# Two of the four combined weight blocks summed on VectorE, one part at a time

## The chip, the cores and the metric

The kernel runs on one core of a Trainium2 chip. A core has a matrix engine (TensorE, PE in the profile), two elementwise engines (VectorE or DVE, ScalarE or ACT), GpSimd (POOL) and SyncE (SP). Here SP only issues DMAs, and POOL mostly issues those that add into their destination or gather rows. Each engine works through a queue of its own, in order; semaphores make one wait for another. The metric is the time of one execution in microseconds of device time. The kernel before took 430.67 us, the median of three runs (430.34 to 432.82).

## The reference

The input `x` is 64 samples of 64 rows and 1024 columns. Each sample picks one of 16 matrices by its condition, and its rows are mixed with it; the mixed rows then go through a dense layer with a mixture of four low-rank experts, and the result is added to `x`:

```python
u = einsum('bct,bcd->bdt', x, weights[condition])      # 64 x 64 per sample
logits = u @ gate_w.T + expert_bias                    # 4 experts
base = einsum('bth,oh->bto', u, W_up)                  # 1024 x 1024
z = einsum('nh,erh->ner', u, lora_A)                   # rank 8 per expert
d = einsum('ner,ehr->neh', z, lora_B)
out = x + base + (d of the expert with the largest logit)
```

All is float32.

## The kernel before

**Order of the algebra.** Mixing rows and multiplying columns commute. The kernel therefore multiplies `x` first with one wide weight matrix, `gate_w`, `lora_A` and `W_up` side by side (1024 x 1060), giving `u`, and mixes the rows of that afterwards, with the block-diagonal matrix `bd` of two samples. Two samples make a tile of 128 rows; there are 32 tiles, and two tiles make a group, so there are 16 groups.

**Precision.** Each operand is split in two parts, a rounded one (`h`, a cast on ACT) and the rest (`l`, a subtraction on DVE, which waits for that cast). A product of two operands is three matmuls: high by high, high by low, low by high. `split_a` (line 124) does this for blocks of `x`, `split_b` (line 141) for blocks of weights, `u_split` (line 186) for `u`.

**Blocks.** A group's 256 rows by 1024 columns of `x` are four blocks A11, A12, A21, A22 and the weights four blocks B11, B12, B21, B22 of 512 by 530. A block of weights is held and split in four parts `k` = 0 to 3, each 128 x 530, 265 KB. A product of two blocks (`product`, line 160) is four steps k of six matmuls, 24 in all. The first two groups need eight products each (`eight`, line 384). The other 14 groups need only seven (`seven`, line 498), by a scheme in the manner of Strassen and Winograd, which uses sums S1 to S4 of the x blocks, made on DVE for each group, and sums of the weight blocks, made once:

T1 = B12 - B11, T2 = B22 - T1, T3 = B22 - B12, T4 = B21 - T2.

These four are made while the first two groups run, since only the third group (`g == 2`) begins to use them: T2 in its second product, T1 in its third, T3 in its fifth, T4 in its seventh.

**How they are made.** `begin_b` (line 145) loads a part of a block into a temporary tile, on SP's queue. `next_b` (line 150) negates a tile in place on ACT and then has POOL issue a DMA that adds a part of another block to it, so every difference is a negation and an accumulating load. T1 starts from a load of B11, T3 from a second load of B12; T2 goes on in T1's tiles, and T4 in T2's. `split_b` then writes the two parts of the result, `hT` and `lT` in the profile. T4's split takes the place of B12's, which is no longer needed.

**Order of the work.** The order of PE, DVE, ACT and POOL is written out by hand: `InOrder` (line 33) keeps the program's order on each of them. In `eight` and `seven`, `at(s, k, fn, ...)` puts a piece of work behind step `k` of product `s` (k = -1: ahead of the product), and `each` does so for several parts. So a position such as (5, 2) says behind which matmuls on PE the work of PE is put, and in which order the other engines find theirs; ACT and DVE do not wait for PE there unless they read something of it. The order of SP's loads follows the program too, and a load waits until the tile that it overwrites is free.

**Around the products.** `u_of` (line 194) takes a finished product out of PSUM (ACT writes `uh`, DVE `ul`). `apply` (line 247) mixes rows: three small matmuls that read `uh` and `ul`. `gate` (line 257) finds the best expert on DVE in seven short instructions, from `lg` to `z`; `turn` (line 276) transposes its result on PE and splits it (`zt`, ACT and then DVE); `delta` (line 290) is one matmul of `zt` with the experts' matrix `b3`; `evict` (line 296) copies the output columns out of PSUM on ACT (`y`), and after a tile's third set of columns POOL adds `x` to it by an accumulating DMA and SP stores it. `finish` (line 311) is `apply`, `delta` and `evict` for one of three sets of columns. `split_b3` (line 366) splits `b3` after its load.

Every tile of weights, S or T is one of ten temporaries of one pool (`tp`, line 81), so a load can wait for an old tile to be read.

Of the kernel before, what the change touches and what calls it, by code (L numbers as in the profile page):

```python
# [17 lines left out]
KH = KC // 2  # L18
# [26 lines left out]
def kernel(  # L45
# [25 lines left out]
    nc = tc.nc  # L71
    NP = x.shape[0]
    NG = NP // 2
    tensor, vector, scalar, pool = (
        InOrder(tc, e) for e in (nc.tensor, nc.vector, nc.scalar, nc.gpsimd)
    )
# [17 lines left out]
    raw, As, us, ys, wsel, zs, os_, ts = ({} for _ in range(8))  # L94

    def temp(name):
        return tp.tile([P, NB], F32, name=name, tag="t")
# [35 lines left out]
    def part(q, k):  # L133
        i, j = int(q[1]) - 1, int(q[2]) - 1
        return w[j][:, KH * i + k]

    def load_b(q, k):
        t = raw[q, k] = temp("wraw")
        nc.sync.dma_start(t, part(q, k))  # L139

    def split_b(q, k):
        scalar.copy(wh[q][:, k], raw[q, k])
        vector.tensor_sub(wl[q][:, k], raw[q, k], wh[q][:, k].bitcast(F32))

    def begin_b(q, k, block):

        t = raw[q, k] = temp(q)
        nc.sync.dma_start(t, part(block, k))

    def next_b(q, k, block, of=None):  # L150

        t = raw[q, k] = raw[of or q, k]
        scalar.mul(t, t, -1.0)
        pool.dma_start(t, part(block, k), accum_op=ALU.add)


    def chain():
# [19 lines left out]
    def body(c):  # L177
        return c[:, LEFT : LEFT + NB]
# [7 lines left out]
    def u_split(i, n, src):  # L186
        h, lo = u_tiles(i)
        scalar.copy(h[:, n], src)
        vector.tensor_sub(lo[:, n], src, h[:, n].bitcast(F32))

    def half(hf):
        return slice(NB * hf, NB * hf + NB)

    def u_of(i, hf, c):
        u_split(i, half(hf), body(c))
# [5 lines left out]
    def u_sum(i, hf, c, t):  # L201
        u_add(i, c, t)
        u_split(i, half(hf), ts["u", i])
# [168 lines left out]
    def run(g, order, hooks, c):  # L372
        for s, (n, l, r, first) in enumerate(order):
            if first:
                c[n] = chain()
            for kk, fn, *args in hooks[s]:
                if kk < 0:
                    fn(*args)
            product(c[n], g, l, r, first, hooks[s])
# [4 lines left out]
    def eight(g):  # L384
        a, b = 2 * g, 2 * g + 1
        h = [[] for _ in range(8)]

        def at(s, k, fn, *args):
            h[s].append((k, fn, *args))

        def each(s, k, fn, q, ks, *args):
            for i in ks:
                at(s, k, fn, q, i, *args)

        one, two = (0, 1), (2, 3)
        if g == 0:
            at(0, 0, split_a, g, "A21")
            each(0, 1, split_b, "B21", one)
            at(0, 2, split_a, g, "A12")
            each(0, 3, split_b, "B21", two)  # L400
            each(1, -1, load_b, "B12", range(KH))
            at(1, 0, split_a, g, "A22")
            each(1, 1, split_b, "B12", one)
            each(1, 3, split_b, "B12", two)
            each(1, 3, load_b, "B22", range(KH))
            at(2, 1, split_cond, a)
            at(2, 2, load_b3)
            for i in (2, 3):
                at(2, 3, load_half, i, 0)
            at(3, -1, lambda: u_of(a, 0, c["1"]))  # L410
            at(3, 1, split_cond, b)
            each(3, 2, split_b, "B22", one)
            each(3, 2, begin_b, "T1", range(KH), "B11")
            at(3, 3, apply, a, 0)
            at(3, 3, gate, a)
            at(4, -1, lambda: u_of(b, 0, c["2"]))
            at(4, 1, split_b3)
            each(4, 2, split_b, "B22", two)
            at(5, 0, turn, a)
            each(5, 0, next_b, "T1", one, "B12")  # L420
            for i in (2, 3):
                at(5, 0, load_half, i, 1)
            at(5, 2, delta, a, 0)
            at(5, 2, evict, a, 0)
            at(6, 0, apply, b, 0)
            at(6, 0, gate, b)
            each(5, 3, next_b, "T1", two, "B12")
            at(5, 3, split_a, g + 1, "A11")
            each(5, 3, begin_b, "T3", range(KH), "B12")
            at(6, 2, split_a, g + 1, "A21")  # L430
            at(6, 3, turn, b)
            at(7, -1, lambda: u_of(a, 1, c["3"]))
            at(7, 1, delta, b, 0)
            at(7, 1, evict, b, 0)
            at(7, 1, split_a, g + 1, "A12")
            at(7, 2, finish, a, 1)
            each(7, 2, split_b, "T1", one)
            at(7, 3, finish, a, 2)
            order = (
                ("1", "A11", "B11", True),  # L440
                ("2", "A21", "B11", True),
                ("1", "A12", "B21", False),
                ("2", "A22", "B21", False),
                ("3", "A11", "B12", True),
                ("1", "A21", "B12", True),
                ("3", "A12", "B22", False),
                ("1", "A22", "B22", False),
            )
        else:
            p = a - 1  # L450
            at(0, -1, lambda: u_of(p, 1, cs[g - 1]["1"]))
            at(0, 0, split_a, g, "A22")
            at(0, 3, finish, p, 1)
            at(1, 0, finish, p, 2)
            each(0, 3, next_b, "T3", (0, 1, 2, 3), "B22")
            each(1, 1, split_b, "T1", two)
            at(1, 1, load_cond, a + 2)
            at(1, 1, load_cond, b + 2)
            for i in (b + 2, a + 2):
                at(1, 1, load_half, i, 0)  # L460
            each(1, 3, next_b, "T2", one, "B22", "T1")
            each(2, 1, next_b, "T2", two, "B22", "T1")
            for i in (b + 2, a + 2):
                at(2, 1, load_half, i, 1)
            at(3, -1, lambda: u_of(a, 1, c["1"]))
            each(3, 1, split_b, "T3", one)
            each(3, 3, split_b, "T3", two)
            at(4, -1, lambda: u_of(b, 1, c["2"]))
            at(4, 0, sums, g + 1, "S1")
            at(4, 1, split_cond, a)  # L470
            each(4, 1, split_b, "T2", one)
            each(4, 2, next_b, "T4", one, "B21", "T2")
            at(4, 3, split_cond, b)
            at(5, 0, sums, g + 1, "S2")
            each(5, 1, split_b, "T2", two)
            each(5, 2, next_b, "T4", two, "B21", "T2")
            at(5, 2, split_a, g + 1, "A11")
            at(5, 3, sums, g + 1, "S3")
            at(6, 1, split_a, g + 1, "S2")
            at(6, 2, sums, g + 1, "S4")  # L480
            at(7, -1, lambda: u_of(a, 0, c["3"]))
            at(7, 3, apply, a, 0)
            at(7, 3, gate, a)
            order = (
                ("1", "A11", "B12", True),
                ("2", "A21", "B12", True),
                ("1", "A12", "B22", False),
                ("2", "A22", "B22", False),
                ("3", "A11", "B11", True),
                ("1", "A21", "B11", True),  # L490
                ("3", "A12", "B21", False),
                ("1", "A22", "B21", False),
            )
        run(g, order, h, c)
        cs[g] = dict(c)


    def seven(g):
        a, b = 2 * g, 2 * g + 1
# [5 lines left out]
        def at(s, k, fn, *args):  # L505
            h[s].append((k, fn, *args))

        def each(s, k, fn, q, ks, *args):
            for i in ks:
                at(s, k, fn, q, i, *args)  # L510
# [15 lines left out]
        if g == 2:  # L526
            at(0, -1, lambda: u_of(pb, 0, cp["1"]))
            at(0, 2, turn, pa)
            at(1, 0, delta, pa, 0)
            at(1, 0, evict, pa, 0)  # L530
            at(1, 1, finish, pa, 1)
            at(1, 2, finish, pa, 2)
            each(1, 3, split_b, "T4", (0, 1))
            each(2, 3, split_b, "T4", (2, 3))
            at(1, 3, apply, pb, 0)
            at(1, 3, gate, pb)
            at(2, 3, turn, pb)
        else:
            at(0, -1, lambda: u_sum(pb, 0, cp["2"], ts["t1"]))
            at(0, 1, finish, pa, 1)  # L540
            at(0, 3, finish, pa, 2)
            at(1, 2, apply, pb, 0)
            at(1, 2, gate, pb)
            at(2, 2, turn, pb)
# [102 lines left out]
    for g in range(2):  # L647
        eight(g)
    for g in range(2, NG):
        seven(g)  # L650
# [44 lines left out]
```

## Time and profile before

| | us |
|---|---|
| median of three runs | 430.67 |
| the profiled execution | 433.13 |
| its span, first to last instruction | 431.1 |
| PE busy in it | 416.1 (97%) |
| DVE busy | 280.3 (65%) |
| ACT busy | 190.5 (44%) |
| POOL busy | 80.3 (19%) |
| DMA of POOL's queue | 21.13 MB, 29.0% of 16 engines' span |
| DMA of SP's queue | 41.53 MB, 27.1% of 16 engines' span |

The profile names instructions by what they write and read: `c<-hT,ah` is a product matmul into the accumulator `c`, `o<-uh,bd` a mixing matmul, `lT<-T,hT` the low part of a combined block. Nearly everything carries line 41, the helper that records it. The page divides the span into 40 slices and prints one digit for each, the busy share in tenths; for PEclk it is the clock that PE was granted. An answer on waits gives the waiting engine and its operation, who ended the wait, and the total, the number and the longest in us. An answer by stretches gives, for each stretch, its length, each engine's busy time with the number of instructions, the granted clock, the DMA share and GB/s. In the timeline a row is the start, the length, the engine, what it did, and in brackets how long the engine had been idle and who ended that.

### The profile page before, as it was taken

The numbers are of one execution on the slowest core, as the hardware profiler recorded it, in microseconds if no ns is written. First come the engines' busy times: TensorE is split into PE (matmuls) and PEld (weight loads), VectorE is DVE, ScalarE is ACT, GpSimd is POOL, SyncE is SP. The second block draws the span as 40 slices with busy tenths as digits, with TensorE's granted clock in tenths as the row PEclk, the third lists the DMA queues.
The fourth block names the chain that finished last, engine by engine and source line by source line (L and its number), as shares of the span: only waits on it lengthen the run. The fifth ranks groups of instructions, "written<-read, shape, count | busy, mean of one in ns | idle before, by whom it ended". The sixth has DMA issues, their size and how long they took to land.

```text
span 431.1 us, 8166 instructions
## 1 busy us (share of the span) xinstructions
PE 416.1 (97%) x3187; PEld 412.6 (96%) x3187; DVE 280.3 (65%) x631; ACT 190.5 (44%) x425; POOL 80.3 (19%) x97
## 2 busy tenths in 40 slices
PE   8979995999999999999999999999999999999996
PEld 6979995999999999999999999999999999999995
DVE  4855355677676766766676666667676666767656
ACT  5764753534353334435234444533444353433531
POOL 3330821302002020200202020110202011020000
PEclk9989997999999999999999999999999999999999
DMA  7999997445354654435465453546445344665343
GB/s 218 344 304 231 221 201 137 79 95 156 106 166 128 172 128 93 126 95 160 129 170 129 100 133 90 157 124 170 129 111 141 89 141 120 173 155 145 50 97 147
DMA packets 26598, 63.18 MB, mean 147 GB/s; under 512 B 3552, under 2 KB 4832, under 8 KB 26560
## 3 DMA queue, kind: packets, MB, share of 16 engines
q0 software_dynamic: 7680, 21.13, 29.0%
q1 hardware_dynamic: 18880, 41.53, 27.1%
q8 instruction: 25, 0.41, 0.4%
q14 instruction: 13, 0.11, 0.1%
HBM read 45.87 MB, written 16.78 MB: 145 GB/s over the span
## 4 chain that ended last, share of the span: by engine, by line
PE 80%; issue 8%; DMA 5%; POOL 3%; DVE 2%; SPq 1%; ACT 1%; POOLq 0%; DVEq 0%
PE c L41 67%; PE o L41 14%; DMA T<-in_w_dram 4%; POOL wsel L41 1%; POOL T L41 1%; DMA cond_sb<-in_cond_dram 1%; DVE lT L41 1%; SPq L327 0%; SPq L139 0%; DVE S L41 0%; ACT hT L41 0%; DVE y L41 0%; DVE al L41 0%; DVE usum L41 0%; DVE ul L41 0%
## 5 line engine op out<-in xcount | busy, mean ns | idle before, releaser
L41 PE MATMUL c<-hT,ah 128*128 128x264 f32 x480 | 140.3, 292 | 0.0
L41 PE MATMUL c<-lT,ah 128*128 128x264 f32 x480 | 137.8, 287 | 0.0
L41 PE MATMUL c<-hT,al 128*128 128x264 f32 x480 | 137.6, 287 | 0.0
L41 PE MATMUL c<-hB,ah 128*128 128x264 f32 (+1 forms) x432 | 125.9, 291 | 0.8 <-ACT ah L41 0.8
L41 PE MATMUL c<-hB,al 128*128 128x264 f32 (+1 forms) x432 | 125.3, 290 | 0.3 <-DVE al L41 0.3
L41 PE MATMUL c<-lB,ah 128*128 128x264 f32 (+1 forms) x432 | 125.0, 289 | 0.3 <-DVE lB L41 0.3
L41 PEld LDWEIGHTS c<-lT,ah 128*128 128x128 f32 x480 | 91.3, 190 | 0.0
L41 PEld LDWEIGHTS c<-hT,al 128*128 128x128 f32 x480 | 91.3, 190 | 0.0
L41 PEld LDWEIGHTS c<-hT,ah 128*128 128x128 f32 x480 | 91.3, 190 | 0.0
L41 PEld LDWEIGHTS c<-hB,ah 128*128 128x128 f32 x432 | 83.1, 192 | 1.5 <-ACT ah L41 1.2
L41 PEld LDWEIGHTS c<-lB,ah 128*128 128x128 f32 x432 | 83.3, 193 | 1.0 <-DVE lB L41 0.9
L41 POOL DMA_DIRECT2D y<-in_x_dram x30 | 28.9, 963 | 293.9 <-ACT y L41 293.9
L41 PEld LDWEIGHTS c<-hB,al 128*128 128x128 f32 x432 | 82.8, 192 | 0.6 <-DVE al L41 0.5
L41 ACT COPY y<-o 128x354 f32<-128x354 f32 (+2 forms) x90 | 39.9, 443 | 62.4 <-PE o L41 60.5
L41 DVE TENSOR_TENSOR al<-xh,ah 128x512 fp32r<-128x512 f32 (+1 forms) x53 | 34.9, 660 | 35.4 <-ACT ah L41 35.4
L41 ACT CAST uh<-usum 128x530 fp32r<-128x530 f32 (+4 forms) x44 | 27.1, 616 | 68.8 <-DVE usum L41 68.7
L41 DVE TENSOR_TENSOR al<-S,ah 128x512 fp32r<-128x512 f32 x56 | 38.5, 688 | 22.9 <-ACT ah L41 22.8
L41 PE MATMUL o<-uh,bd 128*128 128x354 f32 (+2 forms) x188 | 45.9, 325 | 4.0 <-ACT uh L41 3.9
L41 ACT CAST zt<-o 96x128 fp32r<-96x128 f32 x32 | 8.4, 262 | 83.2 <-PE o L41 83.2
L41 DVE TENSOR_TENSOR ul<-usum,uh 128x530 fp32r<-128x530 f32 (+4 forms) x44 | 30.0, 683 | 19.3 <-ACT uh L41 19.3
L41 POOL DMA_INDIRECT wsel<-in_cw_dram,idx x32 | 35.2, 1101 | 9.9 <-issue 4.9
L41 ACT CAST ah<-S 128x512 fp32r<-128x512 f32 x56 | 34.8, 623 | 0.3
(59 smaller groups left out, 461.6 us busy)
## 6 DMA issues: line engine op xcount, KB each, us to landing
xh<-in_xt_dram SPq DMA_DIRECT2D x63, 256.0 KB
y<-in_x_dram POOLq DMA_DIRECT2D x30, 512.0 KB, 5.8
out_dram<-y SPq DMA_DIRECT2D x30, 512.0 KB
wraw<-in_w_dram SPq DMA_DIRECT2D x16, 265.0 KB
T<-in_w_dram POOLq DMA_DIRECT2D x16, 265.0 KB, 7.3
T<-in_w_dram SPq DMA_DIRECT2D x8, 265.0 KB
y<-in_x_dram SPq DMA_DIRECT2D x2, 512.0 KB
wsel<-in_cw_dram,idx POOLq DMA_INDIRECT x32, 5.1
```

The costliest lines, as they stand in the source:

```text
L41: return lambda *a, **k: self.tc.keep_in_program_order(fn(*a, **k))
```

## The change

T1 and T2 are no longer made by negation and accumulating loads. For each part k, `load_two` loads B11 and B12 on SP's queue. `make_t1` subtracts the two on DVE into a tile of its own and splits it. `start_t3` negates the tile of B12 on ACT and has POOL add B22 to it: T3. `make_t2` splits T3, adds it to the tile of B11 on DVE, which is T2 since B11 + B22 - B12 = B22 - T1, and splits that. `start_t4` negates T2's tile and has POOL add B21: T4. SP still loads eight parts, POOL's accumulating loads of weights fall from 16 to eight, and DVE gets eight sums.

The work is put down part by part, from the fifth product of the first group to the seventh of the second, with T4's last two parts split in the third group's second product. Around it several things move: B22's second half is split before `b3`, `turn` of the second tile of group 0 moves from (6, 3) to (7, 0) and its `gate` from (6, 0) to (6, 1), its `delta` from (7, 1) to (7, 2), the first tile's last `finish` goes into group 1, and splits and sums of x blocks move by a step or two. The products and their order stay.

```diff
@@ -142,16 +142,33 @@
         scalar.copy(wh[q][:, k], raw[q, k])
         vector.tensor_sub(wl[q][:, k], raw[q, k], wh[q][:, k].bitcast(F32))
 
-    def begin_b(q, k, block):
-
-        t = raw[q, k] = temp(q)
-        nc.sync.dma_start(t, part(block, k))
-
-    def next_b(q, k, block, of=None):
-
-        t = raw[q, k] = raw[of or q, k]
+
+
+    def load_two(k):
+        load_b("B11", k)
+        load_b("B12", k)
+
+    def make_t1(k):
+        t = raw["T1", k] = temp("T1")
+        vector.tensor_sub(t, raw["B12", k], raw["B11", k])
+        split_b("T1", k)
+
+    def take_from(q, k, block, old):
+        t = raw[q, k] = raw[old, k]
         scalar.mul(t, t, -1.0)
         pool.dma_start(t, part(block, k), accum_op=ALU.add)
+
+    def start_t3(k):
+        take_from("T3", k, "B22", "B12")
+
+    def make_t2(k):
+        split_b("T3", k)
+        t = raw["T2", k] = raw["B11", k]
+        vector.tensor_add(t, raw["T3", k], t)
+        split_b("T2", k)
+
+    def start_t4(k):
+        take_from("T4", k, "B21", "T2")
 
 
     def chain():
@@ -410,32 +427,36 @@
             at(3, -1, lambda: u_of(a, 0, c["1"]))
             at(3, 1, split_cond, b)
             each(3, 2, split_b, "B22", one)
-            each(3, 2, begin_b, "T1", range(KH), "B11")
             at(3, 3, apply, a, 0)
             at(3, 3, gate, a)
             at(4, -1, lambda: u_of(b, 0, c["2"]))
-            at(4, 1, split_b3)
-            each(4, 2, split_b, "B22", two)
+            each(4, 1, split_b, "B22", two)
+            at(4, 2, load_two, 0)
+            at(4, 2, load_two, 1)
             at(5, 0, turn, a)
-            each(5, 0, next_b, "T1", one, "B12")
+            at(5, 0, split_b3)
             for i in (2, 3):
                 at(5, 0, load_half, i, 1)
-            at(5, 2, delta, a, 0)
-            at(5, 2, evict, a, 0)
-            at(6, 0, apply, b, 0)
-            at(6, 0, gate, b)
-            each(5, 3, next_b, "T1", two, "B12")
-            at(5, 3, split_a, g + 1, "A11")
-            each(5, 3, begin_b, "T3", range(KH), "B12")
+            at(5, 1, make_t1, 0)
+            at(5, 1, start_t3, 0)
+            at(5, 2, split_a, g + 1, "A11")
+            at(5, 3, delta, a, 0)
+            at(5, 3, evict, a, 0)
+            at(5, 3, load_two, 2)
+            at(6, 0, make_t1, 1)
+            at(6, 0, start_t3, 1)
+            at(6, 1, apply, b, 0)
+            at(6, 1, gate, b)
             at(6, 2, split_a, g + 1, "A21")
-            at(6, 3, turn, b)
+            at(6, 2, load_two, 3)
             at(7, -1, lambda: u_of(a, 1, c["3"]))
-            at(7, 1, delta, b, 0)
-            at(7, 1, evict, b, 0)
+            at(7, 0, turn, b)
             at(7, 1, split_a, g + 1, "A12")
-            at(7, 2, finish, a, 1)
-            each(7, 2, split_b, "T1", one)
-            at(7, 3, finish, a, 2)
+            at(7, 2, delta, b, 0)
+            at(7, 2, evict, b, 0)
+            at(7, 2, make_t1, 2)
+            at(7, 2, start_t3, 2)
+            at(7, 3, finish, a, 1)
             order = (
                 ("1", "A11", "B11", True),
                 ("2", "A21", "B11", True),
@@ -449,35 +470,36 @@
         else:
             p = a - 1
             at(0, -1, lambda: u_of(p, 1, cs[g - 1]["1"]))
-            at(0, 0, split_a, g, "A22")
+            at(0, 0, finish, p - 1, 2)
+            at(0, 1, split_a, g, "A22")
+            at(0, 2, make_t1, 3)
+            at(0, 2, start_t3, 3)
             at(0, 3, finish, p, 1)
             at(1, 0, finish, p, 2)
-            each(0, 3, next_b, "T3", (0, 1, 2, 3), "B22")
-            each(1, 1, split_b, "T1", two)
             at(1, 1, load_cond, a + 2)
             at(1, 1, load_cond, b + 2)
             for i in (b + 2, a + 2):
                 at(1, 1, load_half, i, 0)
-            each(1, 3, next_b, "T2", one, "B22", "T1")
-            each(2, 1, next_b, "T2", two, "B22", "T1")
-            for i in (b + 2, a + 2):
                 at(2, 1, load_half, i, 1)
+            at(1, 2, make_t2, 0)
+            at(1, 3, start_t4, 0)
+            at(2, 1, make_t2, 1)
+            at(2, 2, start_t4, 1)
             at(3, -1, lambda: u_of(a, 1, c["1"]))
-            each(3, 1, split_b, "T3", one)
-            each(3, 3, split_b, "T3", two)
+            at(3, 2, make_t2, 2)
+            at(3, 3, start_t4, 2)
             at(4, -1, lambda: u_of(b, 1, c["2"]))
             at(4, 0, sums, g + 1, "S1")
             at(4, 1, split_cond, a)
-            each(4, 1, split_b, "T2", one)
-            each(4, 2, next_b, "T4", one, "B21", "T2")
-            at(4, 3, split_cond, b)
+            at(4, 1, split_cond, b)
+            at(4, 2, make_t2, 3)
+            at(4, 3, start_t4, 3)
             at(5, 0, sums, g + 1, "S2")
-            each(5, 1, split_b, "T2", two)
-            each(5, 2, next_b, "T4", two, "B21", "T2")
-            at(5, 2, split_a, g + 1, "A11")
-            at(5, 3, sums, g + 1, "S3")
-            at(6, 1, split_a, g + 1, "S2")
-            at(6, 2, sums, g + 1, "S4")
+            at(5, 1, split_a, g + 1, "A11")
+            at(5, 2, sums, g + 1, "S3")
+            at(6, 0, split_a, g + 1, "S2")
+            at(6, 1, sums, g + 1, "S4")
+            each(6, 2, split_b, "T4", one)
             at(7, -1, lambda: u_of(a, 0, c["3"]))
             at(7, 3, apply, a, 0)
             at(7, 3, gate, a)
@@ -530,8 +552,7 @@
             at(1, 0, evict, pa, 0)
             at(1, 1, finish, pa, 1)
             at(1, 2, finish, pa, 2)
-            each(1, 3, split_b, "T4", (0, 1))
-            each(2, 3, split_b, "T4", (2, 3))
+            each(1, 3, split_b, "T4", (2, 3))
             at(1, 3, apply, pb, 0)
             at(1, 3, gate, pb)
             at(2, 3, turn, pb)
```

## Prediction

> **What bounds the kernel now.** I read the first two parts of the page, then busy time by stretch, then TensorE's waits up to 95 us.
>
> ```profile
> span 431.1 us, 8166 instructions
> PE 416.1 (97%) x3187; PEld 412.6 (96%) x3187; DVE 280.3 (65%) x631; ACT 190.5 (44%) x425; POOL 80.3 (19%) x97
> ...
> PEclk9989997999999999999999999999999999999999
> ```
>
> TensorE (PE) is the bound and its total work stays. The clock row dips in slices three and seven only: early, in the two groups with eight products, which hold the edit. From 87.4 us on the chain repeats every 24.9 us per seven products, without a gap. So I ask what the early waits cost. Stretches in us, busy time and count by engine, granted clock, DMA share, GB/s:
>
> ```profile
> 26.00:29.00 3.00, 0.39 (x1) 0.39 (x2) 2.50 (x4) 1.94 (x5) 1.29 (x2) 0.88 0.85 248
> 29.00:32.00 3.00, 3.00 (x15) 3.00 (x15) 0.68 (x1) 2.53 (x5) 2.09 (x3) 0.55 1.03 368
> ...
> 64.00:68.00 4.00, 0.07 (x2) 0.09 (x1) 2.21 (x4) 3.56 (x7) 1.70 (x2) 1.00 0.91 137
> 68.00:72.00 4.00, 2.52 (x11) 2.23 (x12) 3.07 (x11) 0.30 (x1) 0.00 (x0) 0.65 1.00 214
> 72.00:76.00 4.00, 4.00 (x20) 3.99 (x20) 1.27 (x4) 0.78 (x2) 0.00 (x0) 0.50 0.12 41
> ```
>
> ```profile
> PE o L41 <- ACT uh L41: 3.9, 1, 3.9
> PE o L41 <- DVE zt L41: 3.3, 2, 2.6
> PE o L41 <- DVE ul L41: 1.5, 1, 1.5
> ```
>
> In the timeline of PE, product matmuls start 0.124 us apart at full clock and 0.22 us in the slow stretches. That gives three losses.
> - **A**, group 0: the first `delta` starts 2.91 us after the matmul before it (2.8 lost), then 12 matmuls at 0.22 instead of 0.124: 1.2.
> - **B**, the end of group 1: last product matmul at 63.73, `apply` at 67.94 waiting for `uh`, its last matmul at 69.98 waiting for `ul`, group 2's first product at 70.44. Without waits that product comes 0.65 after 63.73, so 6.1 is lost; then 25 starts at 0.22: 2.4.
> - **C**, group 2: `delta` waits 0.8 for `zt`.
> Together 13.3 us: the ceiling of any gain here.
>
> Behind B stands this, in the timeline of ScalarE (ACT) and that of VectorE (DVE):
>
> ```profile
> 60.25 0.64 ACT L41 CAST hT<-T 128x530 fp32r<-128x530 f32 x1 [0.76 <-DMA T<-in_w_dram]
> 60.79 0.64 ACT L41 ACTIVATE T<-T 128x530 f32<-128x530 f32 x1
> 61.66 0.65 ACT L41 ACTIVATE T<-T 128x530 f32<-128x530 f32 x1 [0.23 <-DVE lT L41]
> ...
> 64.21 0.63 ACT L41 CAST hT<-T 128x530 fp32r<-128x530 f32 x1 [0.84 <-DMA T<-in_w_dram]
> ```
>
> ```profile
> 60.92 0.71 DVE L41 TENSOR_TENSOR lT<-T,hT 128x530 fp32r<-128x530 f32 x1 [0.68 <-ACT hT L41]
> ...
> 69.22 0.70 DVE L41 TENSOR_TENSOR ul<-c,uh 128x530 fp32r<-128x530 f32 x1
> ```
>
> ACT waits for accumulated blocks, and `ah` and `uh` queue behind; then DVE works off al, S, al, S before `ul`. The rows also price a handoff: ACT to DVE 60.25 to 60.92 = 0.67, DVE to ACT 60.92 to 61.66 = 0.74. Back to back, DVE starts 0.62 apart (0.60 for 512 columns), ACT 0.54.
>
> [...]here the 16 accumulating ones took 4.3 to 11.2, median 7.3, and I use those.
>
> **Part by part.**
>
> *DMA and negations.* POOL's accumulating loads fall from 16 to 8, ACT's negations (`ACTIVATE T`) too; SP keeps 8 plain loads in the same places of its queue. That is 2.1 MB less. Off the path in itself. The remaining accumulations are issued far ahead: T3's first starts near 29.3 and is read at 43.3, its last near 42 and read at 57. The longest landing seen, 11.2, fits, so ACT's waits for DMA in B go.
>
> *Eight sums on DVE.* 8 x 0.62 = 5.0 us. Bounds for one: 0.60 (a 512-column S) and 0.71 (the profiled length); none is free, DVE has room (65% busy), but a sum adds two handoffs to its part.
>
> *Group 0, A.* Splitting B22 before `split_b3` frees `zt` from the wait for b3. b3 lands at 24.55 (its cast starts at 24.58 after a DMA wait). DVE: two lB to 25.8, zt, b from 26.1 to 27.35. `delta` is due at the product's end, 26.55: it waits 0.85. Before, 2.8.
>
> *Group 0, new wait.* Behind b, DVE now has, ahead of `gate(b)`: T1 sum at 27.4 (SP's next issues show that its second load lands by about 27.1), hT 28.13, lT 28.8, negation 28.67, ah 29.2, al 29.85, T1 sum 30.45, hT 31.2, lT 31.85, gate 32.5; z is out at 33.95 (a gate takes 1.45 from `lg`). PE reaches `turn(b)` at about 31.8: from `delta` at 27.4, five k-steps of 0.74, `delta` 0.15, `apply` 0.48. It waits 2.15. Group 0's products then end at 36.45, and with `finish(a, 1)`'s 0.65 at 37.1. Before, without `finish(a, 2)`, which moves to group 1, 38.25. So 1.15 is gained, which is just the slow clock of A; the waits only changed place (0.85 + 2.15 for 2.8).
>
> *Group 1, B.* PE runs on: 37.1 + eight products of 2.96 + three finishes of 0.65 = 62.7. ACT takes up the parts of T2 after `y(b, 2)`, at about 43.3. A part is a chain: hT3, +0.67 lT3, +0.62 T2 sum, +0.73 hT2, +0.67 lT2, +0.74 negation, +0.55 next: 3.98 us. Two parts end at 51.25; `uh` 0.5 and 0.15 for DVE at its `ul`; third part ends 55.9; `uh` 0.5, four `bd` casts 1.05, and 0.9 more because DVE has ul, S1 and four bd (0.62 + 0.60 + 1.0) ahead; fourth part ends 62.1. Then ACT has ah, ah, hT4, hT4, uh; DVE has S2 61.4, al 62.7, S3, al, S4, lT4, lT4 and `ul` at 66.35 (done 67.05). PE waits for that `ul`: group 2 starts at 67.3 instead of 70.44, of which 0.3 was slow clock in `apply`. 2.85 gained by waits, A's share in it.
>
> *Clock after B.* Idle from 62.7 to 67.1 with 0.35 of work: [...]1.7 to 3.5 us lost, 2.55 in the middle, against 2.7 before (2.4 + 0.3). Gain about 0.3 (-0.8 to +1.0).
>
> *C.* T4's last parts are split ahead of `gate(pb)`, so 1.33 us of `lT` no longer stands before `zt`: 0.8 gained. Its DMA, issued near 62, is needed near 73: covered even at 11.2.
>
> *Moves at no cost.* `finish(a, 2)` and the last two T1 parts go into group 1's first product: PE does the same 0.65 there, and ACT and DVE have until group 2's third product for T1. Two more splits of T4 in group 1 are not free: they are the lT4 pair ahead of `ul` above, 1.2. SP's queue keeps its order of x halves and stores; POOL's `y` and `wsel` come behind four T3 loads rather than eight, and their readers (stores, `bd` at 56) have over 8 us. If one came late, `bd` would hold ACT's fourth part, one for one.
>
> **Sum.** 2.85 + 0.3 + 0.8 = 4.0 off the profiled execution's 433.13 (span 431.1 and 2.0 around it): 429.1. The median is 430.67, 2.5 lower, and the runs lie 2.5 apart (430.34 to 432.82). [...]where A doesn't trip, the 1.15 is not there to gain. [...]I take 3.3 off the median: **427.4 us**.
>
> **Rivals.**
> - *The slow clock stays away after B*[...]: 2.6 more, 424.8. [...]Chance 0.12.
> - *B goes altogether*: DVE and ACT run the parts closer than I chain them, `ul` comes by 63. Then 4 us of waits and 2.6 of clock go too: 420.8. For: all data is there early. Against: handoffs of 0.67 and 0.74 in every such row. 0.10.
> - *Slower: the T2 parts take longer.* They stand between ACT and DVE from 43 to 62; if other work splits the handoffs so that a part takes 5.5 instead of 4.0, `ul` comes 6 us later and group 2 starts at 73.3: 433.4. From 0.8 more per part nothing is left of the gain. For: DVE's and ACT's queues are in order and have S, bd and u between. Against: I found only 1.05 of it. 0.08.
> - *`turn(b)`'s wait trips the clock*: [...]1.7 lost: 429.1 to 431. 0.10.
>
> **Numbers.** Forecast 0.60, 425.5 to 429.5. Range 423.5 to 431.0, leaving out `B goes altogether` and the slower rival, 0.18. About 1% (4.3 us) is what a measurement of this kernel tells from no change. Faster by more: the first two rivals and 0.14 of the forecast's 0.60, 0.36. Slower by more: under half of the slower rival, 0.04. Within: 0.60.
>
> **What would show it.** POOL with 8 loads of weights and ACT without DMA waits on T3 and T4; a `delta` wait below 1 us near 27; a wait of about 2 us for z near 32; group 2's start near 67 behind `ul`; no wait for `zt` in group 2. I am wrong if `turn(b)` doesn't wait, if group 2 starts before 65 or after 69, or if the stretches from 95 us on change.

## The result

The changed kernel took 429.24 us, the median of seven runs (427.86 to 429.42), the kernel before 432.36 (430.34 to 432.82, seven runs that include the three of above). The ratio is 0.993, with a 95% interval of 0.991 to 0.995. Measured again beside the experiments, it was 429.40, the median of 22 runs, against 431.47 of 45, ratio 0.995 (0.993 to 0.997). The gain is 2.1 to 3.1 us, below one per cent. Forecast were 3.3 us. The time named, 427.4, lies 1.8 below the measured one; 1.7 of that is the amount by which the median of before turned out higher than its first three runs had shown.

### The profile page after: what moved, and what is told of

The parts are those of the page before. It is cut to its first block, busy times and chain, and to the rows that moved or that the text cites. A ratio compares the mean times of both kernels' runs of the same rounds, so it can differ in the third digit from the quotient of the medians.

```text
span 426.1 us, 8141 instructions
## 1 busy us (share of the span) xinstructions
PE 413.4 (97%) x3187; PEld 409.9 (96%) x3187; DVE 285.2 (67%) x639; ACT 186.2 (44%) x417; POOL 73.6 (17%) x89
## 4 chain that ended last, share of the span: by engine, by line
PE 87%; DVE 5%; ACT 3%; DMA 2%; issue 2%; SPq 1%; DVEq 0%; ACTq 0%
PE c L41 72%; PE o L41 15%; DMA wraw<-in_w_dram 2%; DVE lT L41 2%; ACT hT L41 1%; DVE wraw L41 1%; ACT wraw L41 0%; DVE al L41 0%; DVE T L41 0%; DVE S L41 0%; ACT ah L41 0%; ACT uh L41 0%; ACT b L41 0%; DVE y L41 0%; SPq L139 0%
## 5 line engine op out<-in xcount | busy, mean ns | idle before, releaser
L41 POOL DMA_DIRECT2D y<-in_x_dram x30 | 27.6, 919 | 286.0 <-ACT y L41 286.0
```

Source lines behind the costliest of these rows:

```text
L41: return lambda *a, **k: self.tc.keep_in_program_order(fn(*a, **k))
```

## The profile after

The page of the changed kernel, from its first two parts:

```profile
span 426.1 us, 8141 instructions
PE 413.4 (97%) x3187; PEld 409.9 (96%) x3187; DVE 285.2 (67%) x639; ACT 186.2 (44%) x417; POOL 73.6 (17%) x89
...
PEclk9999998999999999999999999999999999999999
```

DVE gained 4.9 us for its eight sums, ACT and POOL lost eight instructions each. The clock row still dips once, in slice seven: group 1's end still waits. The answer on TensorE's waits up to 100 us (the rows left out are waits before 20 us):

```profile
PE o L41 <- DVE z L41: 2.1, 1, 2.1
PE o L41 <- ACT uh L41: 2.0, 1, 2.0
PE o L41 <- DVE ul L41: 1.7, 1, 1.7
...
PE o L41 <- DVE b L41: 0.3, 1, 0.3
```

The wait for `zt` is gone at both places, a short one for `b` and a new one for `z` came, and those for `uh` and `ul` are shorter in total (3.7 us for 5.4). By stretches:

```profile
32.00:36.00 4.00, 1.97 (x16) 2.00 (x17) 3.73 (x11) 2.09 (x6) 0.87 (x1) 1.00 0.95 192
60.00:64.00 4.00, 2.91 (x24) 2.70 (x23) 2.67 (x6) 3.10 (x6) 0.84 (x1) 1.00 0.01 1
64.00:68.00 4.00, 1.42 (x5) 1.16 (x6) 3.25 (x7) 1.28 (x3) 0.00 (x0) 0.85 0.87 197
68.00:72.00 4.00, 4.00 (x27) 4.00 (x26) 1.95 (x8) 0.73 (x2) 0.00 (x0) 0.73 0.02 6
```

The first row is the new wait for `z`, at full clock. From 60 to 64, where the wait at group 1's end begins, the DMA share is 0.01: hardly a transfer runs. What group 1's end waits for is in the timeline of ACT, which shows one part of T2 and T4 (split of T3, split of T2, negation) and the start of the next:

```profile
43.37 0.64 ACT L41 CAST hT<-wraw 128x530 fp32r<-128x530 f32 x1
45.41 0.64 ACT L41 CAST hT<-wraw 128x530 fp32r<-128x530 f32 x1 [1.40 <-DVE wraw L41]
46.83 0.65 ACT L41 ACTIVATE wraw<-wraw 128x530 f32<-128x530 f32 x1 [0.78 <-DVE lT L41]
47.38 0.62 ACT L41 CAST hT<-wraw 128x530 fp32r<-128x530 f32 x1
```

Every idle stretch in a part is now ended by DVE, none by a DMA; this part takes 4.01 us, of which ACT idles 2.18. The end of that chain is in the timeline of DVE:

```profile
60.79 0.71 DVE L41 TENSOR_TENSOR lT<-wraw,hT 128x530 fp32r<-128x530 f32 x1 [0.70 <-ACT hT L41]
61.42 0.68 DVE L41 TENSOR_TENSOR S<-S,xh 128x512 f32<-128x512 f32 x1
...
65.15 1.32 DVE L41 TENSOR_TENSOR lT<-wraw,hT 128x530 fp32r<-128x530 f32 x2
66.39 0.70 DVE L41 TENSOR_TENSOR ul<-c,uh 128x530 fp32r<-128x530 f32 x1
```

`ul` starts at 66.39, where 66.35 was worked out, and group 2's first product at 67.60.

The profiles do not reach the same place of the program at the same moment of their spans: the first transpose of group 0 lies up to 1.0 us apart. So I measure from this transpose, which on TensorE stands ahead of the first wait that differs, to group 2's first product, and call it the **early stretch**. Its two ends on TensorE, first in the kernel before, then in the changed one:

```profile
24.23 0.27 PE L41 MATMUL o<-ident,z 128*96 128x128 f32 x1
70.44 0.42 PE L41 MATMUL c<-hB,ah 128*128 128x264 f32 x1
...
24.48 0.27 PE L41 MATMUL o<-ident,z 128*96 128x128 f32 x1
67.60 0.42 PE L41 MATMUL c<-hB,ah 128*128 128x264 f32 x1
```

That is 46.2 us before and 43.1 after. The changed kernel's second profile, of the run named `again`, has 42.9: there half clock (a granted clock of 0.50) set in a little later, behind group 2's first matmuls, whose starts are 0.12 to 0.13 us apart from 67.31 and 0.22 from 67.74.

> The changed kernel once more, as the base for the runs beside it. Both theories: 427.9 to 429.4 us, group 2's first product near 67.6 us, 2.1 us of waiting for z at the second tile's turn, 2.0 for uh and 1.7 for ul at the end of group 1.

It gave 429.40 us, the median of 22 runs, and the same waits within 0.1 us.

## The experiments

The first three runs were measured beside `again`. The last four form a second set, in which the kernel before took 431.05 us (59 runs) where the first set has 431.47. The changed kernel was not measured in that set, so a difference between one of these four and its 429.40 can be off by about the 0.4 us between the sets.

**T1's second part behind the gate.** Takes the work that the forecast had found ahead of `gate(b)` out of its way.

```diff
-            at(6, 0, make_t1, 1)
-            at(6, 0, start_t3, 1)
             at(6, 1, apply, b, 0)
             at(6, 1, gate, b)
...
-            at(7, 2, make_t1, 2)
-            at(7, 2, start_t3, 2)
+            at(7, 2, make_t1, 1)
+            at(7, 2, start_t3, 1)
...
+            at(0, 1, make_t1, 2)
+            at(0, 1, start_t3, 2)
             at(0, 2, make_t1, 3)
```

> T1's second part no longer stands ahead of the gate of group 0's second tile; it is made behind that tile's delta, the third part in group 1's first product. Both theories: the 2.1 us wait for z goes. Theory one (the prediction's: the T2 parts start when TensorE has passed group 1's first finishes, so what TensorE wins there carries through): group 2 starts about 2.1 us earlier, near 65.5. Theory two (the chain of T1 and T2 parts on ScalarE and VectorE is continuous from 34 us on and TensorE only waits for it elsewhere): T2's first part starts near 42.9 instead of 43.4, group 2 starts near 67.1, and the time falls by 0.5 us or less, with a longer wait for uh and ul at group 1's end.

428.23 us (eight runs), 1.2 below the changed kernel. The early stretch is 42.6, only 0.5 shorter, with 2.1 us of waiting gone. Two of its waits, at group 1's end:

```profile
PE o L41 <- ACT uh L41: 3.1, 1, 3.1
PE o L41 <- DVE ul L41: 1.7, 1, 1.7
```

The wait for `z` is not in the answer, and the one for `uh` grew from 2.0 to 3.1. T2's first part starts on ACT at 42.87 instead of 43.37. So theory two holds for the early stretch: from the turn on, ACT and DVE have a queue of T parts that TensorE's gain hardly starts earlier. It had set 0.5 us as the most to be gained, though, and the median fell by 1.2. The profile doesn't show the rest: its execution took 428.48 us, more than the 427.86 of the changed kernel's, since half clock at group 1's end lasted 6.83 us (65.19 to 72.02) rather than 3.41 (66.76 to 70.18). The fastest runs of the two kernels are alike, 427.82 and 427.75; but none of these eight took more than 428.48, while 14 of the changed kernel's 22 took 429.21 or more. What those 14 lost is not in a profile.

**T2's parts in pairs.** The same instructions, in an order in which one part's handoff hides another's work.

```diff
-    def make_t2(k):
-        split_b("T3", k)
-        t = raw["T2", k] = raw["B11", k]
-        vector.tensor_add(t, raw["T3", k], t)
-        split_b("T2", k)
+    def make_t2(*ks):
+        for k in ks:
+            split_b("T3", k)
+        for k in ks:
+            t = raw["T2", k] = raw["B11", k]
+            vector.tensor_add(t, raw["T3", k], t)
+        for k in ks:
+            split_b("T2", k)
...
-            at(1, 2, make_t2, 0)
-            at(1, 3, start_t4, 0)
-            at(2, 1, make_t2, 1)
-            at(2, 2, start_t4, 1)
+            at(1, 2, make_t2, 0, 1)
+            at(2, 1, start_t4, 0)
+            at(2, 1, start_t4, 1)
...
-            at(3, 2, make_t2, 2)
-            at(3, 3, start_t4, 2)
+            at(3, 2, make_t2, 2, 3)
+            at(3, 3, start_t4, 2)
+            at(3, 3, start_t4, 3)
...
-            at(4, 2, make_t2, 3)
-            at(4, 3, start_t4, 3)
```

> T2's parts are made two at a time: both T3 splits, both sums, both T2 splits, both negations. Theory of the serial handoffs: a pair takes about 5.2 us instead of 2 x 3.98, so the chain ends 5.5 us earlier, ul is done before TensorE asks for it, the waits for uh and ul (2.0 and 1.7) and the half clock behind them go: group 2 starts near 63.4 and the time falls by 4 to 6.5 us. Rival (the accumulating loads are what the chain stands on): the second pair waits for T3's last part, issued at 42.6 and read near 50, and the gain stays below 2 us.

423.18 us (six runs), ratio to the kernel before 0.982 (0.978 to 0.985), 6.2 us below the changed kernel. The timeline of ACT over one pair:

```profile
43.01 1.18 ACT L41 CAST hT<-wraw 128x530 fp32r<-128x530 f32 x2
45.67 1.26 ACT L41 CAST hT<-wraw 128x530 fp32r<-128x530 f32 x2 [1.48 <-DVE wraw L41]
47.09 1.27 ACT L41 ACTIVATE wraw<-wraw 128x530 f32<-128x530 f32 x2 [0.16 <-issue]
48.26 0.58 ACT L41 CAST uh<-c 128x530 fp32r<-128x530 f32 x1
```

That is 5.25 us for two parts, where two single ones took 8.0. TensorE's waits between 20 and 100 us are then these two alone, and from 56 to 76 us it is busy throughout, at full clock:

```profile
PE o L41 <- DVE z L41: 2.1, 1, 2.1
PE o L41 <- DVE b L41: 0.3, 1, 0.3
```

The early stretch is 38.8, 4.4 shorter. The two profiled executions are 5.9 us apart (427.86 and 421.97): besides the 4.4, 1.2 come behind the early stretch, where 12 starts at 0.22 us are gone, and 0.4 ahead of it, where this execution was earlier. The serial handoffs were the bound of group 1's end, and the second pair did not wait for its accumulating load, so the rival fails.

**One more sum in each part of T2.** The opposite: the suspected cost, made longer.

```diff
+        vector.tensor_add(temp("idle"), raw["T3", k], t)
         vector.tensor_add(t, raw["T3", k], t)
```

> One more VectorE sum of the same size ahead of each of the four T2 sums, its result unused. Theory of the serial handoffs: each part takes 0.62 us longer, so ul and group 2's start come 2.5 us later (near 70.1) and the time rises by 2.5 us, half clock apart. Rival (VectorE has room, 67% busy, or the loads set the pace): 0.5 us or less.

432.88 us (22 runs), 3.5 above the changed kernel. A part now takes 4.76 us (45.49 to 50.25 on ACT), 0.75 longer rather than 0.62, since the second sum follows the first only after 0.74; four times that is 3.0. From T2's first part to group 2's first product it is 27.2 us, where the changed kernel took 24.2, so these 3.0 are all there. In this profile the early stretch grew by 4.5, to 47.6. The other 1.5 came ahead of the parts: here the wait for `z`, as long as ever (2.1 us), was followed by half clock, as these stretches show:

```profile
32.53:35.94 3.41, 1.31 (x11) 1.34 (x12) 3.17 (x10) 2.13 (x5) 0.87 (x1) 1.00 0.99 211
35.94:39.35 3.41, 3.41 (x16) 3.41 (x15) 2.11 (x4) 1.61 (x3) 0.47 (x1) 0.50 0.73 199
```

Up to T2's first part this is the changed kernel's own program, so the same can happen in an execution of that one. A longer part is paid in full, and the rival that expected 0.5 us falls.

**No accumulating loads of weights.**

```diff
         scalar.mul(t, t, -1.0)
-        pool.dma_start(t, part(block, k), accum_op=ALU.add)
```

> The changed kernel without its eight accumulating loads of weights; T3 is then only the negated B12 and T4 the negated T2, so the sums that use them are left out. Theory of the serial handoffs: every such load lands well before it is read, so nothing moves: within 0.7 us of the changed kernel, group 2 starts at 67.5. Rival (fewer accumulating loads are what the change gained by): taking away the other eight gains again, 2 us or more.

429.40 us (22 runs), as the changed kernel took in the other set; the early stretch is 42.9, and the waits are the same. The eight loads that are left cost nothing here.

**b3 later, alone.** The kernel before with one part of the change.

```diff
-            at(4, 1, split_b3)
-            each(4, 2, split_b, "B22", two)
+            each(4, 1, split_b, "B22", two)
             at(5, 0, turn, a)
+            at(5, 0, split_b3)
```

> The kernel before with one part of the change alone: B22's second half is split ahead of b3, and b3 behind the first turn. Both theories: the wait at the first delta falls from 2.6 to about 0.4 us and the half clock behind it goes, 3.5 us at that place. If the end of group 1 follows TensorE, group 2 starts 3.5 us earlier and the time falls by 3 to 3.5 us. If it stands on the accumulating loads and ScalarE's waits for them, group 2 starts within 1 us of 70.4 as before, and the time stays within 1 us.

430.16 us (22 runs), ratio to the kernel before 0.998 (0.996 to 0.999): 0.9 us. `delta` waits 1.07 us in its profile, for `b`, at the earlier place (5, 2); nothing runs slow behind it, as product matmuls start 0.12 to 0.13 us apart from 27.76 on. Of the waits of ACT, 30 to 80 us, this one counts:

```profile
ACT hT L41 <- DMA T<-in_w_dram: 6.9, 6, 2.9
```

ACT still waits 6.9 us for accumulated blocks, and TensorE 3.6 for `uh` and 1.3 for `ul`. Yet its early stretch is 43.3, and the changed kernel's 43.1. The two ways of making T1 and T2 therefore brought group 2 to its start at nearly the same time: the waits for DMA that the change removed were made up by the waits of ACT and DVE for each other.

Neither forecast came whole. The early stretch is 2.9 us shorter than in the profile of before, and its execution took 3.0 less (430.16 and 433.13), as if the end of group 1 followed TensorE; the median fell by 0.9 only, since the profiled execution of before was a slow one among its own runs. In this set the run without accumulation, which took as long as the changed kernel, lies 0.8 below this one. That is all that is left for the rest of the change, and about what the vanished wait for `zt` in group 2 (C) is worth. So no gain of the sums on DVE themselves shows. A run with the new T1 and T2 and the old place of `b3` would settle it; there is none.

**T4's splits ahead of the gate, alone.** The other part, on the kernel before.

```diff
-            each(1, 3, split_b, "T4", (0, 1))
-            each(2, 3, split_b, "T4", (2, 3))
+            each(1, 3, split_b, "T4", (0, 1, 2, 3))
```

> The kernel before with another part alone: all four T4 splits ahead of the gate in group 2's second product. Theory: the 0.64 us wait for zt near 87 goes and the time falls by 0.6 to 0.8 us. Rival (a wait that comes back later): no change.

431.17 us (22 runs), ratio 1.000 (0.999 to 1.002): nothing. The wait for `zt` went, and a new one came ahead of it, as the answer on waits says:

```profile
PE o L41 <- DVE zt L41: 1.8, 1, 1.8
PE o L41 <- DVE ul L41: 1.1, 1, 1.1
PE o L41 <- DVE z L41: 1.0, 1, 1.0
```

The first row is group 0's `delta`, the third the new wait in group 2, at 83.36. DVE has four `lT` (2.58 us in one row) ahead of the gate, so `z` comes late where `zt` came late before. The change has no wait at this place; it also took two of the four splits out of group 2, into group 1, where they stand ahead of `ul`. That these two make the difference is worked out, from 1.3 us of `lT` less ahead of a wait of 1.0, and not tried alone.

This run shows one thing more. Up to group 2 it is the kernel before, and its first `delta` waits 1.8 us, not the 2.6 of the profile of before; the early stretch is 44.9, not 46.2. So the loss A was larger in that one execution than in this one.

**Both orders together.** Pairs, T1's second part behind the gate, and T4's first two splits behind the gate of group 1's first tile:

```diff
-            each(6, 2, split_b, "T4", one)
...
             at(7, 3, apply, a, 0)
             at(7, 3, gate, a)
+            each(7, 3, split_b, "T4", one)
```

> T2's parts in pairs and T1's second part behind the gate together, and T4's first two splits put behind the gate of group 1's first tile. With the waits at the end of group 1 gone, what TensorE wins at the turn should now carry through, under either theory of the single edits: group 2 starts near 60.8, 2.1 us earlier than with pairs alone, and the time is near 421, below both kernels. If VectorE's ul at the end of group 1 becomes late again, up to 1 us of it is lost.

420.64 us (six runs, 420.24 to 420.84), ratio to the kernel before 0.977 (0.974 to 0.979), 8.8 us below the changed kernel's 429.40. Between 20 and 100 us one wait is left, and the clock row of its page is even:

```profile
PE o L41 <- DVE b L41: 0.3, 1, 0.3
```

```profile
PEclk9999999999999999999999999999999999999999
```

The early stretch is 36.7, 2.0 shorter than with pairs alone. The wait for `z`, which was worth 0.5 us in that stretch while the T2 chain was the bound, is worth its full 2 us once it isn't. The new place of T4's splits is part of this run too, and was not tried without the rest.

## Why the prediction was right

- *A.* Forecast 0.85 us lost at `delta`; 0.5 measured by the starts on TensorE (the idle time shown is 0.35). `zt` at 25.1 and b at 26.0 came a little earlier than worked out. The loss before was mis-sized for a median: 4.0 us stood in the one profile, but the run with T4's splits alone, whose program is the same there, shows 1.8 of waiting for 2.6, and b3 later alone gained 0.9.
- *The new wait at the turn.* Forecast 2.15, measured 2.12; the gate began at 32.51, worked out was 32.5. It had no line of its own in the profile of before and came out of queue order and durations.
- *B.* Forecast: `uh` and `ul` still late, group 2's start at 67.3. Measured 67.60. That accumulating loads would be in time held: their landing took 4.3 to 6.9 us, and the run without them moved nothing. (The prediction's own terms for the fourth part add up to 62.3, not the 62.1 written; 62.09 was measured.) What doesn't follow is that the new way of making T1 and T2 earned these 2.85 us against the old: with `b3` moved alone, the old way's early stretch is within 0.2 us of the new one's.
- *What starts the T2 chain.* Here a step fails: "PE runs on ... ACT takes up the parts of T2 after `y(b, 2)`". In the changed kernel this gives the right time, 43.3 for 43.37. But the run with T1 behind the gate brought TensorE 2.1 us earlier and the chain only 0.5: ACT reaches that place late by itself. TensorE and ACT arrive within half a microsecond of each other, so a gain of TensorE beyond that is lost, while a delay of it counts in full (the 1.5 us at the turn in the kernel with the extra sum). So the step "2.85 gained by waits, A's share in it" fails in the changed kernel: what TensorE gains by A doesn't carry through to group 2.
- *The clock after B.* Forecast 1.7 to 3.5 us lost; about 1.5 in the profile (12 starts and a slow `apply`), and 25 starts before. The gain by it was 1.2 us in these two profiles rather than 0.3. That the clock would fall after the idle time was the author's estimate; it fell to 0.50, for 3.41 us here (66.76 to 70.18) and for 6.83 before (69.22 to 76.05). Half of each, 1.7 and 3.4, is about the range forecast. Which of the two an execution gets was not shown: the run with T1 behind the gate had 6.83 again.
- *C.* The wait of 0.8 us is gone in the changed kernel, but not by the cause named. To put T4's last parts ahead of `gate(pb)` does nothing alone; as worked out at that run, the other two splits have to leave the group too.
- *The sum.* 3.3 off the median forecast, 3.1 and 2.1 measured in two sets. That it came so close is in part luck. Between the profiled executions 4.0 were worked out and 5.3 measured (433.13 to 427.86): that of before was slower than any of the seven runs, that of the changed kernel the fastest of its seven. And the size of A, the cause given for B, and C's cause were off as said.
- *The rivals.* The slow clock did not stay away, B didn't go (with T2's parts in pairs it does), a part took 4.0 us, and at the turn half clock followed in the profile with the extra sum (0.50 from 35.94 to 39.35) but not in the changed kernel's (1.00). The slower rival has its mechanism shown by the extra sum: 0.75 more per part made the kernel 3.5 us slower and cost the gain, where 0.8 had been the point named.

## What to carry to other kernels

When a transfer is replaced by work of two engines, count the handoffs and not only the busy time: ACT idled 2.2 of 4.0 us in a part, and the same instructions in pairs were worth 6.2 us, more than the change itself. A wait on the busiest engine may be slack of a longer queue elsewhere; before it is removed, ask which chain reaches the next meeting point last. Moving work ahead of one late reader puts it in front of another: walk the queue to the next reader as well. And try the small parts of a change alone: moving `b3` gave 0.9 us with none of the new sums.

## What was not expected of the hardware

- Two waits of the same 2.12 us for `z` cost differently in clock. In the trace of the kernel before, the granted clock is 0.50 from 28.27 to 31.68 us and from 69.22 to 76.05, so for 3.41 us and for 6.83. Between the two it is 1.00 for 37.55, which is 11 times 3.413. Stretches of this length, laid on its changes of clock:

```profile
24.86:28.27 3.41, 1.12 (x10) 0.91 (x8) 2.54 (x3) 3.08 (x6) 0.56 (x1) 1.00 0.90 261
28.27:31.68 3.41, 3.06 (x13) 3.07 (x14) 0.65 (x2) 2.40 (x5) 2.50 (x4) 0.50 1.01 364
...
62.40:65.81 3.41, 1.61 (x14) 1.40 (x12) 2.46 (x5) 2.29 (x6) 1.14 (x3) 1.00 0.81 112
65.81:69.22 3.41, 0.56 (x2) 0.30 (x2) 2.41 (x4) 2.49 (x5) 1.58 (x2) 1.00 0.91 137
69.22:72.63 3.41, 2.65 (x11) 2.65 (x12) 2.48 (x9) 0.00 (x0) 0.00 (x0) 0.50 0.91 234
72.63:76.05 3.42, 3.42 (x17) 3.41 (x17) 0.69 (x3) 0.78 (x2) 0.00 (x0) 0.50 0.03 9
```

  In the changed kernel half clock begins at 66.76, and an estimate of where such stretches lie earlier, by steps of 3.413 back from there, puts an edge at 32.63, inside the wait for `z` (31.91 to 34.03). Both stretches beside it had full clock:

```profile
29.22:32.63 3.41, 2.69 (x21) 2.47 (x20) 2.33 (x5) 2.35 (x5) 1.05 (x2) 1.00 1.01 306
32.63:36.04 3.41, 2.01 (x17) 2.04 (x18) 3.17 (x10) 1.50 (x5) 0.82 (x1) 1.00 0.99 199
```

  In the kernel with the extra sum the same wait (32.51 to 34.63) lay almost whole in one stretch, 32.53 to 35.94, and half clock followed until 39.35. These rows agree with the place of the wait making the difference, which was not tried alone. Half clock followed 2.29 us (24.86 to 28.27) and 2.85 (65.81 to 69.22) of idle TensorE in one such stretch of the kernel before, and 2.85 in the changed one (63.35 to 66.76); of two stretches with 1.8 it followed one (25.85 to 29.26 with T4's splits alone) and not the other (62.40 to 65.81 in the kernel before). Half clock lasted 3.41 us in the two cases where TensorE was busy for 3.06 us (28.27 to 31.68, before) and 3.04 (66.76 to 70.18, changed) of it, and 6.83 where it was busy for 2.65 of the first 3.41 (69.22 to 72.63, before).
- The times of a kernel went with the mean clock of its runs. The kernel with both orders, whose mean clock was 0.999 to 1.000, spread over 0.6 us in six runs; the changed kernel, 0.987 to 0.996, over 4.2 in 22. Its eight runs at 0.995 or 0.996, the profiled execution of `again` among them, took 428.83 us or less, the other 14 at least 429.21. The estimate for 3.41 us of half clock is 0.004 of the mean of such a span (half of 3.41 in 426 us), so 0.996 would be one time 3.41, and 0.992 and 0.988 two and three; the profile of the kernel before has 3.41 and 6.83 at a mean of 0.988. One profile shows one of these cases, and a forecast made from it inherits that.
- In the kernel with the extra sum, where the second sum overwrites what the first reads, the two start 0.74 us apart in all four parts (46.79 and 47.53 in the first); back to back and independent, DVE's instructions of this size start 0.62 apart. That the overwriting is the reason was not tried.
